# A two-layer decoder on one core: mask product issued once, silu as tanh, tables and gates earlier, a new order in the second attention

## The chip, the cores and the metric

The kernel runs on one core of a Trainium2 chip. Its time is the device time of one execution in microseconds (us). The core has five engines that each take their instructions strictly in order: PE (TensorE, matrix products and transposes; its weight loads are listed as PEld), DVE (VectorE), ACT (ScalarE), POOL (GpSimd) and SP (SyncE, which issues most DMAs). They wait for one another through semaphores. The kernel's work is described in the order of its Python code, and a scheduler fixes the order in which each engine gets its instructions when the program is built, so a change of the code can move instructions that it does not mention.

## The reference

Everything is float32. Four sequences of 256 tokens, 256 wide, go through two decoder layers; each layer adds three blocks to `x`, with a layer norm before each.

```python
x = x + L0_attn(ln(x))            # 8 heads, 2 key/value heads, 32 wide, window of 64, tanh soft cap
x = x + L0_xattn(ctx, ln(x))      # state-space scan over ctx (16 states), gated by silu(ln(x))
x = x + L0_ffn(ln(x))             # 704 wide, silu(g) * u
x = x + L1_attn(ln(x))            # 16 heads, 4 key/value heads, 128 wide, causal
x = x + L1_xattn(ctx, ln(x))      # a second scan, gated
x = x + L1_ffn(ln(x))             # 32 experts, 6 chosen for each token, and a shared one
```

The parts that the change touches, cut to the core:

```python
# L0_attn, after rotating q and k and normalising q, k and v
scores = jnp.where(allowed, q @ k.T / sqrt(D), -inf)
probs = softmax(tanh(scores / 30) * 30)
# scan: for each time step t, with 256 channels and 16 states
state = state * exp(d_t * A) + (d_t * u_t) * B_t
y_t = (state @ C_t) + D * u_t           # then y * silu(z), z = ln(x)
# L0_ffn
g = (xf @ gate_w.T) * gate_s
u = (xf @ up_w.T) * up_s
out = ((silu(g) * u) @ down_w.T) * down_s
# L1_attn
q = layernorm(q, qn_g, qn_b);  k = layernorm(k, kn_g, kn_b)
q = q * cos + rotate_half(q) * sin      # the same for k
weights = softmax(where(causal, -inf, q @ k.T / sqrt(D)))
x_add = concat_heads(weights @ v) @ w_o.T
```

## The kernel before

`x` lies in SBUF for the whole program, eight blocks of 128 tokens. The work runs through these stages, and the two scans are threaded through the others as generators that yield after each state.

**Layer 0's attention** (from L340, batches 0 to 3). `head0` normalises and projects a batch and rotates q and k: for each half `c` of the batch it writes the product with cos to SBUF, the product of the swapped halves with sin to SBUF, and after both halves one add over both joins them. `tail0` makes the scores. For each of two key/value heads and each pair of heads it takes two PSUM tiles, puts the window's mask into them as a product of an identity with the table `far` (bfloat16, L432), and then adds the score products (L436) on top. The mask product runs three times in a row into the same two tiles; each starts the tile afresh, so the last one alone decides what lies there. Then ACT takes tanh and exp, PE the weighted values, DVE divides.

**The scan** (`mamba_front` from L150, `mamba_scan` from L202). For each state and half of the channels: ACT takes an exponential into PSUM (`h`, L215), POOL forms `db` (L217), DVE runs the scan in place (L218) and multiplies by C (`hc`, L220). In layer 0 PE sums the even states in PSUM by a product with the identity (L235) and POOL adds the odd ones to `y` (L237); in layer 1 POOL adds all (L227). The front of a scan also uses silu (`u`), softplus (`dt`) and exp (`negA`) on ACT. Where ACT goes from a function of one table set to one of another, the program has a table load, which the profile lists as an ACT row without a tile.

**The gate** (`mamba_gate`, L246). For a batch: layer-norm statistics of `x` (DVE, then four small POOL steps), silu on ACT (`sz`, L252), a product with the scan's `y` on DVE (`yg`), four transposes (L258), an add to `x` (L264).

**Feed-forward** (L541 to L587). Two halves of two batches each. A half gates its batches, normalises and transposes them, and runs six chunks of the inner width (`ic`). Each chunk has two PSUM tiles, gate `pg` and up `pu`, from a pool of two (`pb`); L554 fills them with four matmuls of 512 columns each for gate and up (a float32 product is two passes); ACT takes silu of `pg` with the gate's scale (L562), and DVE multiplies it by `pu` and the up scale into `hT` (L565). Then the down matmuls (L578, 48 records) and the add to `x` (L586). The second half begins once the layer-0 scan `s01` has run to its end.

**Second attention** (L590 to L821, loop L1009 to L1029). At its start POOL builds the rotary tables with the norms' weights folded in (`cg`, `sg`, `bt`, L602 to L621), PE transposes one of them (L629), and the mean of the q and k weights over a head has been taken out (`wmean`, L520 to L524, one reduce over all 20 heads, and two subtractions on POOL). For each batch `keys_values` (L687) normalises the batch, projects and rotates its keys. For each of its four key/value heads, a step, `queries` (L680) projects, rotates and transposes both halves of four query heads: `rotate` (L652) takes squares on ACT (L658) and three passes on DVE (L663, L670, L671), `transposed` (L674) four transposes (L677) and a copy. `rsqrt` (L632) is one step on DVE (L635) and a power on POOL (L636). `scores` (L735) makes scores (L741, L750), adds offsets and mask on DVE (L759), takes the negative maximum (`nm`), the exponential with its sum on ACT (L769), the reciprocal of the sums on DVE (L772), and scales on POOL (L774). `weighted` (L777) transposes (L784 the first) and multiplies with the values; `project_out` (L807) runs after every second step and adds to `x` (L820). The loop keeps two steps in flight, in this order:

```python
xnT, kT = keys_values(b)
for g in range(NKV1):
    rq = queries(xnT, g, qT)
    queued.append((b, g, qT, rq, kT, xnT))
    if len(queued) > 1: score()
    if len(scored) > 1: finish()
    with tc.issue_after(pace[-3]) ...: run(states, ...)   # some states of layer 1's scan
```

`score` makes the scores of the step before, `finish` the weighting of the step before that. `pace` holds the reciprocals, and the scan's states of a step may not be issued before the third last of them.

**Mixture of experts** (`moe`, from L904): for each expert up (L944), gate and square (L949, L950) and down (L958). Its routing and first products begin before the second attention ends.

## Time and profile before

| | us |
|---|---|
| median of 3 runs | 913.7 (910.06 to 918.71) |
| the profiled execution | 913.37 |
| its span | 911.6 |
| mean granted clock of PE | 0.941 |

Busy time over the span: PE 805.6 us (88%), its weight loads 500.7, DVE 585.5 (64%), ACT 485.9 (53%), POOL 422.3 (46%). A busy time counts records from start to end, and those of PE overlap and are modelled, so PE at 88% is not PE at its peak. Averages over the whole span say little here, since each stage has another limit. The stages lie about so: layer 0's attention 0 to 200, feed-forward 212 to 314 (first half 212 to 257, second 279 to 314), second attention 321 to 665, experts 665 to the end.

The chain of waits, which follows the work that ended last back from the end, gives PE 52% of the span, DVE 15%, ACT 7%, POOL 5% and starts for which nothing was waited 4%. The page's groups of instructions have one row for a line, engine and shape: count, busy time, mean duration in ns, then the idle time of that engine just before, and who ended most of it. In a list of the chain, the columns are the start and the length in us, then engine, tile, line and count.

### The profile page before, as it was taken

What the parts mean: (1) busy time and instruction counts of PE and PEld (TensorE: products, weight loads), DVE (VectorE), ACT (ScalarE), POOL (GpSimd) and SP (SyncE); (2) the same over time, 40 slices, a digit from 0 to 9 for tenths busy, and PEclk for the clock granted to TensorE, in tenths of its full rate; (3) what the DMA queues carried; (4) which work ended last, traced back from release to release, by engine and by line L of the source; (5) the groups of instructions that cost most, each with busy time, mean ns of one, the idle gap of its engine ahead of it and who ended that gap; (6) DMA issues with size and microseconds to landing.
All of it is one profiled execution on the core that took longest, in us unless ns stands there. A gap on an engine that the chain in (4) does not pass through costs nothing.

```text
span 911.6 us, 10272 instructions
## 1 busy us (share of the span) xinstructions
PE 805.6 (88%) x3074; PEld 500.7 (55%) x3074; DVE 585.5 (64%) x1096; ACT 485.9 (53%) x1191; POOL 422.3 (46%) x421
## 2 busy tenths in 40 slices
PE   4888789978968789889898978997999999999997
PEld 1444456633434435646564755675666656666665
DVE  3799797677867268979669874777256776221221
ACT  2768453778869346757765664776523343211111
POOL 3366866467759334847656652332347661000000
PEclk9999787987988989999999989997999999999999
DMA  4357354464532200101111110000137653555442
GB/s 160 117 152 268 105 184 162 145 216 152 200 115 92 86 30 24 46 24 47 46 47 56 38 35 12 24 3 1 49 116 228 226 151 112 159 143 154 161 148 81
DMA packets 60999, 98.36 MB, mean 108 GB/s; under 512 B 6336, under 2 KB 26704, under 8 KB 60688
## 3 DMA queue, kind: packets, MB, share of 16 engines
q1 hardware_dynamic: 59232, 95.77, 33.0%
q10 hardware_dynamic: 1712, 1.94, 0.7%
q8 instruction: 24, 0.39, 0.2%
q14 instruction: 31, 0.25, 0.1%
HBM read 96.24 MB, written 1.44 MB: 107 GB/s over the span
## 4 chain that ended last, share of the span: by engine, by line
PE 52%; DVE 15%; ACT 7%; POOL 5%; issue 4%; DMA 1%; POOLq 0%; SPq 0%; DVEq 0%; ACTq 0%
PE ps L944 12%; PE ps L958 12%; PE ps L812 5%; PE ps L554 4%; PE ps L643 4%; PE ps L578 2%; PE ps L750 2%; DVE h L218 2%; PE ps L797 2%; DVE ps L670 1%; DVE qs L663 1%; ACT sc L769 1%; DVE hc L220 1%; DVE qr L671 1%; PE ps L677 1%
## 5 line engine op out<-in xcount | busy, mean ns | idle before, releaser
L217 POOL TENSOR_TENSOR db<-bt,du 128x512 f32<-128x512 f32 x128 | 163.5, 1290 | 86.6 <-DVE h L218 64.3
L218 DVE TENSOR_TENSOR_SCAN h<-h,db 128x512 f32<-128x512 f32 x128 | 152.5, 1216 | 17.6 <-ACT h L215 16.0
L958 PE MATMUL ps<-w,hT 128*128 128x256 f32 x544 | 128.8, 380 | 0.0
L944 PE MATMUL ps<-moe_xnT,w 128*128 128x512 f32 x272 | 128.8, 597 | 0.0
L949 DVE SCALAR_TENSOR_TENSOR hT<-ps,gr 128x512 f32<-128x512 f32 x64 | 44.1, 689 | 127.0 <-PE ps L944 127.0
L958 PEld LDWEIGHTS ps<-w,hT 128*128 128x128 f32 x544 | 103.3, 191 | 40.3 <-issue 29.4
L215 ACT ACTIVATE h<-dt,negA 128x512 f32<-128x512 f32 x128 | 86.5, 689 | 62.6 <-DVE hc L220 61.9
L950 ACT ACTIVATE hT<-hT 128x512 f32<-128x512 f32 x68 | 42.8, 629 | 134.1 <-DVE hT L949 133.9
L643 PE MATMUL ps<-wqkv,xnT 128*128 128x512 f32 x192 | 95.7, 611 | 7.6 <-DVE rq L635 4.1
L220 DVE TENSOR_TENSOR hc<-h,ct 128x512 f32<-128x512 f32 x128 | 84.9, 679 | 4.1 <-POOL y L237 2.1
L227 POOL TENSOR_TENSOR y<-y,hc 128x512 f32<-128x512 f32 x64 | 80.8, 1272 | 8.0 <-DVE hc L220 8.0
L636 POOL TENSOR_TENSOR rq<-rq,nhalf 128x8 f32<-128x8 f32 x20 | 33.0, 1648 | 90.6 <-DVE rq L635 90.4
L944 PEld LDWEIGHTS ps<-moe_xnT,w 128*128 128x128 f32 x272 | 51.7, 191 | 36.5 <-issue 33.2
L658 ACT ACTIVATE sq<-ps 128x128 f32<-128x128 f32 x160 | 42.4, 282 | 41.3 <-PE ps L643 37.9
L769 ACT ACTIVATE sc<-sc,nm 128x256 f32<-128x256 f32 (+1 forms) x128 | 56.7, 449 | 12.3 <-DVE nm L764 8.2
L774 POOL TENSOR_TENSOR sc<-sc,rsum 128x512 f32<-128x512 f32 (+1 forms) x32 | 46.3, 1468 | 35.3 <-DVE rsum L772 33.6
L812 PE MATMUL ps<-wo,oT 128*128 128x256 f32 x256 | 57.0, 381 | 0.4 <-ACT oT L805 0.4
L812 PEld LDWEIGHTS ps<-wo,oT 128*128 128x128 f32 x256 | 48.1, 190 | 9.2 <-ACT oT L805 2.6
L235 PE MATMUL ps<-hc,ident 128*128 128x512 f32 x64 | 39.9, 712 | 13.9 <-DVE hc L220 10.9
L643 PEld LDWEIGHTS ps<-wqkv,xnT 128*128 128x128 f32 x192 | 33.8, 195 | 30.3 <-issue 20.7
L677 PE MATMUL ps<-ident,qr 128*128 128x128 f32 x160 | 28.9, 299 | 18.4 <-DVE qr L671 16.2
L237 POOL TENSOR_TENSOR y<-y,hc 128x512 f32<-128x512 f32 x32 | 40.8, 1275 | 7.6 <-DVE hc L220 6.3
(200 smaller groups left out, 1449.2 us busy)
## 6 DMA issues: line engine op xcount, KB each, us to landing
bt<-bc SPq DMA_DIRECT2D x96, 256.0 KB, 3.5
ct<-bc SPq DMA_DIRECT2D x96, 256.0 KB, 3.6
w<-in_w_dram SPq DMA_DIRECT2D x64, 256.0 KB, 3.6
gr<-gt SPq DMA_DIRECT2D x64, 256.0 KB, 3.5
wqkv<-in_wqkv_dram SPq DMA_DIRECT2D x1, 3072.0 KB, 14.1
wo<-in_wo_dram SPq DMA_DIRECT2D x1, 2048.0 KB, 8.1
x<-in_x_dram SPq DMA_DIRECT2D x4, 256.0 KB, 5.3
w<-in_ws_dram SPq DMA_DIRECT2D x4, 256.0 KB, 3.2
```

Source lines behind the costliest of these rows:

```text
L215: nc.scalar.activation(h, dt[:, c, :], AF.Exp, scale=negA[:, a : a + 1])
L217: nc.gpsimd.tensor_mul(db, bt, du[:, c, :])
L218: nc.vector.tensor_tensor_scan(h, h, db, 0.0, ALU.mult, ALU.add)
L220: nc.vector.tensor_mul(hc, h, ct)
L227: nc.gpsimd.tensor_add(y[:, c, :], y[:, c, :], state(n, c, bt, ct))
L643: mm(pq, lhsT=xnT[:, f, c * P : (c + 1) * P], rhs=wqkv1[:, f, ch * 512 : (ch + 1) * 512], start=(f == 0), stop=(f == 1),)
L769: nc.scalar.activation(part, part, AF.Exp, bias=nm[:, qc, j : j + 1], accum_out=rsum[:, qc, j : j + 1])
L774: nc.gpsimd.tensor_mul(part, part, rsum[:, qc, :].unsqueeze(2).to_broadcast([P, 4, w]))
L812: mm(pout[:, c * 256 : (c + 1) * 256], lhsT=oTs[h // 4][:, h % 4, c * P : (c + 1) * P], rhs=wo1[:, 8 * gp + h, :], start=(h == 0), stop=(h ...
L944: mm(ph_, lhsT=w[:, f * P : (f + 1) * P], rhs=xnT[:, f, :], start=(f == 0), stop=(f == 1))
L949: gated.append(nc.vector.scalar_tensor_tensor(h, ph_, 0.0, g, ALU.max, ALU.mult).ins)
L958: mm(po[t // 2][:, (t % 2) * 256 : (t % 2 + 1) * 256], lhsT=h[:, t * P : (t + 1) * P], rhs=w[:, 256:512], start=start and t % 2 == 0, stop ...
```

## The change

The mask product in `tail0` is issued once instead of three times. The rotation of layer 0 multiplies by cos in place in PSUM and adds for each half. The rotary tables of the second attention are built before feed-forward's code, in a pool that lives for the whole program, and the weights' mean is taken in four pieces of five heads. `mamba_gate` is split: `gates_of` has the statistics and the silu, and in feed-forward both batches' `gates_of` stand ahead of the rest of `s01`. Feed-forward's silu becomes a tanh: silu(g) is g/2 times (1 + tanh(g/2)), so ACT takes a tanh with half the scale, a new DVE step forms (1 + tanh) times `pg`, and the multiplier of the last step is the product of half the gate's scale and the up scale (`both`). In the second attention `queries` rotates both halves before it transposes either; `keys_values` of the next batch is called after step 1 of a batch; the reciprocal of the sums is a power of −1 on POOL, and `pace` takes the second maximum instead; the add to `x` after `project_out` is put off to the start of the next `finish` (`settle`).

Left out of the diff below are a renamed constant (`R_KG` is `R_1`, the same column) and the list `owed` among the loop's lists.

```diff
@@ -95,2 +95,4 @@
     nc.gpsimd.memset(nhalf, -0.5)
+    minus = cpool.tile([P, 8], F32, name="minus")
+    nc.gpsimd.memset(minus, -1.0)
     dpool = ctx.enter_context(tc.tile_pool(name="dpool", bufs=1, space=bass.MemoryType.DRAM))
@@ -245,13 +247,20 @@
-    def mamba_gate(l, b, pool):
+    def gates_of(b, pool, bufs):
         nb, rs = ln_stats([x[:, 2 * b + c, :] for c in range(2)])
-        pt = ps(pool)
+        szs = []
         for c in range(2):
-            sz = work.tile([P, S], F32, tag="sz", name="sz")
+            szs.append(pool.tile([P, S], F32, tag="sz", name="sz", bufs=bufs))
             nc.scalar.activation(
-                sz, x[:, 2 * b + c, :], AF.Silu, bias=nb[:, c : c + 1], scale=rs[:, c : c + 1]
+                szs[c], x[:, 2 * b + c, :], AF.Silu, bias=nb[:, c : c + 1], scale=rs[:, c : c + 1]
             )
+        return szs
+    def mamba_gate(l, b, pool, szs=None):
+        szs = szs or gates_of(b, work, 2)
+        pt = ps(pool)
+        for c in range(2):
             yg = work.tile([P, S], F32, tag="yg", name="yg")
-            nc.vector.tensor_mul(yg, y_of[l, b // 2][:, c, (b % 2) * S : (b % 2 + 1) * S], sz)
+            nc.vector.tensor_mul(yg, y_of[l, b // 2][:, c, (b % 2) * S : (b % 2 + 1) * S], szs[c])
             for lh in range(2):
@@ -358,3 +367,2 @@
                 q3 = pq[:, 0:320].rearrange("p (h d) -> p h d", d=32)
-                nc.vector.tensor_mul(r[:, c, 0:10, :], q3, cos.unsqueeze(1).to_broadcast([P, 10, 32]))
                 nc.vector.tensor_mul(
@@ -364,2 +372,5 @@
                 )
+                nc.vector.tensor_mul(q3, q3, cos.unsqueeze(1).to_broadcast([P, 10, 32]))
+                nc.vector.tensor_add(r[:, c, 0:10, :], q3, rr[:, c])
                 nc.scalar.copy(
@@ -367,3 +378,2 @@
                 )
-            nc.vector.tensor_add(r[:, :, 0:10, :], r[:, :, 0:10, :], rr)
@@ -427,7 +437,4 @@
                     psc = [ps(pb) for _ in range(2)]
-                    for last in range(3):
-                        for p_ in psc:
-                            mm(p_[:, 0:320], lhsT=identb, rhs=far, start=True, stop=(last < 2))
+                    for p_ in psc:
+                        mm(p_[:, 0:320], lhsT=identb, rhs=far, start=True, stop=False)
                     for klo, qlo, lo, hi in ((0, 0, 0, NEAR), (P, P, NEAR, 320)):
@@ -518,8 +525,34 @@
+    tabs = []
+    for gcol, bcol in ((R_QG, R_QB), (R_1, R_KB)):
+        g_ = row[:, gcol - R_BR : gcol - R_BR + D1]
+        b_ = row[:, bcol - R_BR : bcol - R_BR + D1]
+        cg = cpool.tile([P, 2, D1], F32, name=f"cg{gcol}")
+        sg = cpool.tile([P, 2, D1], F32, name=f"sg{gcol}")
+        bt = cpool.tile([P, 2, D1], F32, name=f"bt{gcol}")
+        bs = cpool.tile([P, 2, D1], F32, tag="bs", name="bs")
+        cos = cst1[:, 0:256].rearrange("p (c d) -> p c d", c=2)
+        sin = cst1[:, C_SIN1 - C_COS1 : C_SIN1 - C_COS1 + 256].rearrange("p (c d) -> p c d", c=2)
+        nc.gpsimd.tensor_mul(cg, cos, g_.unsqueeze(1).to_broadcast([P, 2, D1]))
+        nc.gpsimd.tensor_mul(bt, cos, b_.unsqueeze(1).to_broadcast([P, 2, D1]))
+        for lo, hi in ((0, 64), (64, 0)):
+            for dst, v in ((sg, g_), (bs, b_)):
+                nc.gpsimd.tensor_mul(
+                    dst[:, :, lo : lo + 64],
+                    sin[:, :, lo : lo + 64],
+                    v[:, hi : hi + 64].unsqueeze(1).to_broadcast([P, 2, 64]),
+                )
+        nc.gpsimd.tensor_add(bt, bt, bs)
+        tabs.append((cg, sg, bt))
     wh = wqkv1[:, :, 0 : 20 * D1].rearrange("p f (h d) -> p f h d", d=D1)
     wmean = cpool.tile([P, 2, 20], F32, name="wmean")
-    nc.vector.tensor_reduce(wmean, wh, AX.X, ALU.add)
-    nc.vector.tensor_scalar(wmean, wmean, 1.0 / D1, None, ALU.mult)
-    for f in range(2):
-        nc.gpsimd.tensor_sub(wh[:, f], wh[:, f], wmean[:, f, :].unsqueeze(2).to_broadcast([P, 20, D1]))
+    for h in range(0, 20, 5):
+        hs = slice(h, h + 5)
+        nc.vector.tensor_reduce(wmean[:, :, hs], wh[:, :, hs], AX.X, ALU.add)
+        nc.vector.tensor_scalar(wmean[:, :, hs], wmean[:, :, hs], 1.0 / D1, None, ALU.mult)
+        for f in range(2):
+            nc.gpsimd.tensor_sub(
+                wh[:, f, hs], wh[:, f, hs], wmean[:, f, hs].unsqueeze(2).to_broadcast([P, 5, D1])
+            )
@@ -538,2 +571,8 @@
+        halfg = wp.tile([P, NIC], F32, name="halfg")
+        both = wp.tile([P, NIC], F32, name="both")
+        nc.gpsimd.tensor_scalar(halfg, par[:, P_GATES : P_GATES + NIC], 0.5, None, ALU.mult)
+        nc.gpsimd.tensor_mul(both, halfg, par[:, P_UPS : P_UPS + NIC])
         conv_taps(1)
@@ -541,2 +580,3 @@
         for hf in range(2):
+            szs = [gates_of(2 * hf + bb, fp, 4) for bb in range(2)]
             if hf == 1:
@@ -545,3 +585,3 @@
             for bb in range(2):
-                mamba_gate(0, 2 * hf + bb, pc)
+                mamba_gate(0, 2 * hf + bb, pc, szs[bb])
                 ln_transposed(2 * hf + bb, xnT[:, :, bb * S : (bb + 1) * S], pc)
@@ -560,13 +600,11 @@
                         )
                 sg = fp.tile([P, 512], F32, tag="sg", name="sg")
-                nc.scalar.activation(
-                    sg[0:m, :], pg[0:m, :], AF.Silu, scale=par[0:m, P_GATES + ic : P_GATES + ic + 1]
+                nc.scalar.activation(sg[0:m, :], pg[0:m, :], AF.Tanh, scale=halfg[0:m, ic : ic + 1])
+                nc.vector.scalar_tensor_tensor(
+                    sg[0:m, :], sg[0:m, :], 1.0, pg[0:m, :], ALU.add, ALU.mult
                 )
                 nc.vector.scalar_tensor_tensor(
-                    hT[0:m, ic, :],
-                    pu[0:m, :],
-                    par[0:m, P_UPS + ic : P_UPS + ic + 1],
-                    sg[0:m, :],
-                    ALU.mult,
-                    ALU.mult,
+                    hT[0:m, ic, :], pu[0:m, :], both[0:m, ic : ic + 1], sg[0:m, :], ALU.mult, ALU.mult
                 )
@@ -599,24 +637,2 @@
-        tabs = []
-        for gcol, bcol in ((R_QG, R_QB), (R_KG, R_KB)):
-            g_ = row[:, gcol - R_BR : gcol - R_BR + D1]
...
-            tabs.append((cg, sg, bt))
         mask1 = cst1[:, C_MASK1 - C_COS1 : C_MASK1 - C_COS1 + 384]
@@ -679,8 +695,7 @@
-        def queries(xnT, g, qT):
+        def queries(xnT, g):
             ss = small.tile([P, 2, 4], F32, tag="qss", name="qss")
-            for c in range(2):
-                transposed(rotate(xnT, c, g, ss[:, c, :]), c, qT)
-            return rsqrt(ss, qks)
+            qrs = [rotate(xnT, c, g, ss[:, c, :]) for c in range(2)]
+            return qrs, rsqrt(ss, qks)
@@ -764,3 +779,3 @@
             nc.vector.tensor_reduce(nm[:, 0, :], sc[:, :, 0:P], AX.X, ALU.max, negate=True)
-            nc.vector.tensor_reduce(nm[:, 1, :], sc[:, :, P:384], AX.X, ALU.max, negate=True)
+            pace.append(nc.vector.tensor_reduce(nm[:, 1, :], sc[:, :, P:384], AX.X, ALU.max, negate=True).ins)
             rsum = small.tile([P, 2, 4], F32, tag="rsum", name="rsum")
@@ -771,3 +786,3 @@
                     )
-            pace.append(nc.vector.reciprocal(rsum, rsum).ins)
+            nc.gpsimd.tensor_tensor(rsum, rsum, minus[:, 0:8].rearrange("p (c h) -> p c h", c=2), ALU.pow)
             for qc, part, w in ((0, sc[:, :, 0:P], P), (1, sc[:, :, P:384], 256)):
@@ -818,4 +833,8 @@
                     )
-            xb = x[:, 2 * b : 2 * b + 2, :]
-            nc.vector.tensor_add(xb, xb, pout.rearrange("p (t d) -> p t d", t=2))
+            owed.append((x[:, 2 * b : 2 * b + 2, :], pout))
+        def settle():
+            for xb, pout in owed:
+                nc.vector.tensor_add(xb, xb, pout.rearrange("p (t d) -> p t d", t=2))
+            owed.clear()
@@ -1008,12 +1028,17 @@
         ready = None
+        keyed = [keys_values(0)]
         for b in range(B):
-            xnT, kT = keys_values(b)
+            xnT, kT = keyed.pop(0)
             for g in range(NKV1):
+                qrs, rq = queries(xnT, g)
                 qT = ap.tile([P, 4, S], F32, tag="qT", name="qT", bufs=2)
-                rq = queries(xnT, g, qT)
-                queued.append((b, g, qT, rq, kT, xnT))
-                if len(queued) > 1:
+                for c in range(2):
+                    transposed(qrs[c], c, qT)
+                if queued:
                     score()
+                queued.append((b, g, qT, rq, kT, xnT))
                 if len(scored) > 1:
                     finish()
+                if g == 1 and b + 1 < B:
+                    keyed.append(keys_values(b + 1))
                 step = 4 * b + g
@@ -1024,2 +1049,3 @@
                 if step == 12:
+                    settle()
                     for bb in range(2):
@@ -1034,2 +1060,3 @@
             finish()
+        settle()
```

By count the built program goes from 1834 to 1770 matmul instructions, from 71 to 40 table loads on ACT, from 26 to 10 reciprocals on DVE and from 349 to 372 two-operand steps on POOL; DVE gets twelve more of the product that the tanh needs. The DMAs are the same in number. In the built order of POOL the tables' 14 steps stand between the first layer norms and the first `krep` of layer 0's attention.

## The prediction

> **What bounds the kernel now.** I read the page's slices first, then windows cut at the stage borders, then the chain of waits inside the stages that the change touches. The slices (each 22.8 us) say which engine fills which stage:
> ```profile
> PE   4888789978968789889898978997999999999997
> ...
> DVE  3799797677867268979669874777256776221221
> ...
> PEclk9999787987988989999999989997999999999999
> ```
> PE carries most of the span, but only the last third (mixture of experts, which the change leaves alone) is solid. Windows by stage; columns are length, then busy time (x instructions) of PE, its weight loads, DVE, ACT and POOL, then granted clock:
> ```profile
> 40.00:100.00 60.00, 49.22 (x210) 26.75 (x211) 58.91 (x94) 43.61 (x79) 37.20 (x36) 0.95 0.59 195
> 100.00:140.00 40.00, 32.86 (x159) 21.76 (x157) 32.35 (x51) 16.26 (x36) 31.93 (x24) 0.80 0.47 155
> 140.00:182.00 42.00, 40.40 (x222) 27.46 (x222) 27.94 (x39) 25.34 (x53) 23.35 (x19) 0.90 0.48 156
> 212.00:257.00 45.00, 44.12 (x118) 21.70 (x118) 37.39 (x45) 38.29 (x45) 33.58 (x29) 0.95 0.62 203
> 257.00:279.00 22.00, 11.44 (x28) 3.91 (x28) 14.35 (x38) 15.14 (x22) 10.43 (x26) 0.67 0.22 67
> 279.00:314.00 35.00, 33.95 (x96) 17.12 (x94) 17.70 (x24) 24.68 (x26) 20.86 (x20) 0.96 0.18 60
> 321.00:595.00 274.00, 242.96 (x987) 155.57 (x988) 210.81 (x401) 174.85 (x654) 147.86 (x126) 0.96 0.11 33
> ```
> So DVE bounds 40-100 (58.9 of 60), PE bounds 140-182 and both feed-forward halves (212-257, 279-314), the gap between the halves (257-279) is latency, with PE busy for half of it at clock 0.67, and in attention 1 PE idles 274 − 243 = 31 us with no other engine full. Times below are against the profiled execution: span 911.6, 913.4 with what lies around it, 0.3 under the median 913.7.
>
> **Mask product.** 64 of 96 products go. The chain shows six of them pipelined, 0.135 each:
> ```profile
> 171.98 0.81 PE ps L432 x6
> ```
> That is 64 × 0.135 = 8.6 us of PE work. Only in 140-182 is PE the bound; about half of the products lie there: 32 × 0.135 = 4.3, of which some is returned as waits on ACT's tanh. I take −3; bounds −8.6 (all on the path) and, leaving the clock to a rival below, 0.
> In-place rotation: one add per batch (1.19 us) becomes two of about 0.48 (the row of the multiplies beside it): −0.24 × 4 = −1 us of DVE, inside the uncertainty of the −3. The mean of the second attention's weights (a 5.46 us reduce, two 4.46 us subtractions) is cut in four with the same elements: no sum changes; the pieces sit among scan states, and were that cover gone, the most is eight more instruction starts, under 1 us.
>
> **Feed-forward, silu as tanh.** ACT now swaps function tables for every inner chunk, because scan's exponentials lie between silus:
> ```profile
> 227.48 1.28 ACT L562
> ...
> 229.49 1.28 ACT L215
> 230.78 0.70 ACT h L215
> ```
> In the whole program 71 loads become 40 by the built code's count, 31 × 1.283 = 39.8 us of ACT, nowhere the fullest engine. On the path stands one stretch in the first half: PE ends at 227.42 and starts again at 234.56 (two loads, sg, h, then DVE's scan), 7.1 us; the half's opening L554 x8 takes 5.79 where later ones take 3.43, 2.4 more for the clock. Against it: each chunk gains one DVE product in two steps, 12 × 0.75 (L565's row) = 9.0 us, and the gate's PSUM buffer, one of two, is held for tanh 0.69 + 0.75 = 1.44, against the 1.72 that PE needs for the other half of the chunk: it fits by 0.28, if DVE comes at once. Queued on DVE ahead of it may be a scan step (h 1.22, hc 0.68); behind it scan steps wait 0.75 each time, and for those PE's state sums (L235) and POOL's. In the built order of after, the states sit behind the first half's L554, and more run in the gap.
> The gap: early gates take two sz, three table loads (1.28 each) and a second statistics chain out of the 17.9 us from 260.40 to 278.29; about 5 us, less what DVE puts between (three h and two hc by the order, 5.0). DVE's floor for 212-279 is 51.7 + 6 × 0.75 = 56.2 of 67, so −11 is the most this stretch could give while DVE is full. I take −6; and for the second half (PE's matmuls fill all but 1.9 of 35; its last chunk trades a 1.28 load for a 0.75 product) −1.5. Bounds for both: −15, and +10 (9.0 of products wholly on the path, plus 1).
>
> [...]
>
> **Tables of the second attention.** At the border PE waits for 14 POOL steps, two transposes, and only then projects:
> ```profile
> 314.25 0.73 POOL cg L611
> ...
> 317.98 0.69 POOL bt L620
> ...
> 318.72 0.69 PE ps L629 x2
> ...
> 321.06 1.22 PE ps L643
> ```
> After's order has the 14 steps at POOL's start, ahead of the first krep, where POOL waits 18.7 us for DVE; they are about 7.5 us and are covered; without the cover they'd delay the scan's first db by as much. Their two DMAs keep their place on ACT's queue. L629 and the layer norm of batch 0 move into the second half's PE stream; what is next is L643 straight after the last L578. Of 314.14 to 321.06 = 6.9 I take −6.5; bounds −7 and −4.5 (layer norm 318.72 to 321.06 stays).
>
> **Second attention's order.** A batch starts with keys, all in one chain:
> ```profile
> 388.49 1.73 PE ps L643 x4
> ...
> 390.30 1.15 ACT sq L658 x8
> ...
> 394.06 1.66 POOL rq L636
> ...
> 397.70 1.10 PE ps L643 x2
> ```
> PE's chain is broken from 390.22 to 397.70, 7.5 us; three times (batches 1 to 3) 22.5. With keys projected a step and a half earlier other PE work covers them. The keys' own instructions (DVE about 10 us a batch: four passes of 0.70 and 0.60 each, eight L696 of 0.3) stay, and stand on DVE and ACT ahead of that step's scan. I take two thirds, −15. The reciprocal leaves DVE, where it waited 17.6 us in all for ACT's exponentials with rotations queued behind it; some reach PE (L677 waits 16.2 on qr): −5. Both rotations ahead of both transposes keep PE's second projection off the first's wait; small, inside this. The add to x, issued a step later, stands in the order right ahead of L759s that need PE's next work anyway: 0; were that cover gone, 8 adds of 0.70 either way, 5.6, inside the bounds. Sum −20. Bounds: all idle PE time of 321-665, 31 + 7.6 = −38.6, and +8 (L677 waiting half as long again, since it now needs both rotations).
> The reciprocal on POOL has this row as nearest (same size, power):
> ```profile
> L636 POOL TENSOR_TENSOR rq<-rq,nhalf 128x8 f32<-128x8 f32 x20 | 33.0, 1648 | 90.6 <-DVE rq L635 90.4
> ```
> 16 × 1.65 = 26.4 us; POOL is at 148 of 274, and the scaled scores usually lie ready 8 us before PE takes them (end 431.6, L784 at 440.07). Behind it on POOL wait the scaling and scan's db. At the last step nothing covers it (L784 waits 1.54 for POOL at 648.37): +1.6; bounds 0 and +3.3 (two steps).
>
> **Sum**: −3 − 6 − 1.5 − 6.5 − 20 + 1.6 = −35.4; 913.4 − 35.4 = 878.
>
> **Rivals.**
> Stalls go wholly: attention at −38.6 instead of −20, and −3 more in feed-forward: 913.4 − 57 = 856. For it: no engine there is full. Against: DVE, in one order, meets PE four times a step.
> Order brings nothing in the second attention: the next wait (qs on sq, scores on DVE) takes the place of the keys' chain. Left are −6.5, −3 in feed-forward and −3, +1.6: 902.5. For it: L820, L677, L735 all end on DVE, which keeps its 211 us.
> No change: attention turns +8, tables and gates pay for it: about 912.
> Slower, the clock: the two extra rounds of mask products also keep PE busy while ACT works. In 40-182 PE is busy 122.5 us at a mean 0.89. At 0.55 the same work takes 122.5 × 0.89 / 0.55 = 198, 56 over the 142 there is; less the other 32 gained, 913.4 + 24 = 937. It decides from the point where the loss is 32: 122.5 × 0.89 / 174 = a granted clock of 0.63. For it: 100-140 is already at 0.80, 257-279 at 0.67. Against: only 8.6 us of work goes, and half the stage waits for DVE, not PE.
> [...]
>
> **How the numbers follow.** Chances: forecast (865 to 893) 0.48, stalls go wholly 0.14, nothing from the order (894 to 909) 0.20, no change 0.06, clock 0.12. A measurement of this kernel tells about 1% from no change, 904.3 and 922.5. Faster: 0.48 + 0.14 + 0.15 = 0.77; within: 0.05 + 0.06 + 0.01 = 0.12; slower 0.11. The range takes in all but the deepest cases below (0.04) and the clock and part of no change above (0.16): 850 to 912.
>
> **What would show it.** Right: PE's first L643 of the second attention follows the last down product within 2 us; periods from one batch's first project_out to the next (428.69, 512.88, 595.14: 84.2 and 82.3) fall to about 77; the gap between the halves is under 15 us; no L562 loads in ACT's row. Wrong: PE waits on DVE's new product in L554, by more than 0.3 a chunk; granted clock under 0.7 in 100-182; key projections stuck behind DVE, so that PE idles mid-batch for as long as it did at the border; PE L784 waiting for POOL in more than two steps.

## The result, and the profile after

| | before | changed |
|---|---|---|
| median of the runs | 915.8 us (4 runs) | 926.0 us (4 runs) |
| ratio to before | 1 | 1.013, 95% interval 1.008 to 1.018 |
| span of the profiled execution | 911.6 us | 926.3 us |
| its mean granted clock of PE | 0.941 | 0.922 |

The changed kernel is 1.3% slower; the forecast was 3.9% faster, and the time lies above the range. The page's slices (each 23.2 us) and the shares of its chain:

```profile
PE   4898999978974987898798889997899999999997
...
DVE  4699785757768458988797587767237676312211
...
PEclk9988766969975999999999999997999999999999
...
PE 50%; DVE 14%; POOL 13%; issue 7%; ACT 3%; DMA 2%; SPq 0%; POOLq 0%; DVEq 0%; ACTq 0%
```

Two things stand out beside the page of before: the 7, 6, 6 in the clock's row between 93 and 162 us, where before has 7, 8, 7; and POOL at 13% of the chain, before 5%. To place the difference I laid the starts and ends of the same instructions of both traces side by side (us from the start of the span):

| | before | changed | moved by |
|---|---|---|---|
| last add of layer 0's attention | 186.5 | 182.0 | −4.5 |
| first half's first up product | 212.6 | 204.5 | −8.1 |
| first half's last down product ends | 257.1 | 246.2 | −10.9 |
| the layer-0 scan's four sums into `y`: second | 158.3 | 162.5 | +4.2 |
| third | 220.4 | 240.6 | +20.2 |
| fourth | 260.4 | 275.8 | +15.4 |
| second half's first up product | 278.3 | 295.5 | +17.2 |
| second half's last down product ends | 314.1 | 332.1 | +18.0 |
| second attention's first projection | 321.1 | 332.9 | +11.9 |
| its last output product ends | 664.9 | 679.8 | +14.9 |
| end of the span | 911.6 | 926.3 | +14.7 |

So attention and the first half did get earlier, by as much as 11 us. It is given back with interest in the gap between the halves, which grew from 21.2 to 49.3 us, because the second half waits for the scan to be finished, and the scan was late. The border to the second attention gave what was forecast, 7.0 to 0.8 us, and the second attention lost 3. In all +18.0 − 6.1 + 3.0, and −0.2 in the experts, make the 14.7 us of the span. In windows (length, then busy time (x instructions) of PE, weight loads, DVE, ACT and POOL, then granted clock, DMA share, GB/s):

```profile
100.00:160.00 60.00, 56.53 (x230) 39.39 (x230) 44.97 (x73) 25.91 (x66) 38.33 (x33) 0.63 0.45 139
204.00:249.00 45.00, 41.89 (x111) 19.56 (x109) 30.91 (x39) 16.50 (x25) 22.44 (x20) 0.95 0.43 133
249.00:276.00 27.00, 18.61 (x33) 6.59 (x32) 18.53 (x24) 15.09 (x19) 20.19 (x17) 0.82 0.56 198
276.00:295.50 19.50, 5.76 (x16) 2.25 (x15) 16.13 (x35) 10.26 (x17) 12.77 (x21) 0.50 0.51 182
333.00:605.00 272.00, 236.63 (x978) 149.12 (x978) 214.23 (x391) 170.96 (x650) 165.06 (x135) 0.99 0.11 34
```

In the first half (204 to 249) DVE is busy for 31 of 45 us, where before it was busy for 37: there was room for scan steps (the in-place scan on DVE, L220), but only 7 stand among the half's products, 10 before. The others stand in 249 to 276. Then 276 to 295.5 is nearly empty of PE work at clock 0.50. The chain there (start, length, what):

```profile
278.32 0.69 DVE x L273
...
282.50 1.09 ACT xn L138 x2
...
284.81 1.24 DVE h L220
...
286.13 1.26 POOL db L219
287.39 1.23 POOL y L229
288.62 1.24 POOL db L219
...
290.24 3.94 DMA w<-in_ws_dram
...
294.40 0.60 ACT xn L138
...
295.52 2.08 PE ps L594 x2
```

L229 is the scan of layer 1. Its first states already stand on POOL's and DVE's queues ahead of the layer norm of the last batch, which the second half needs. The chain's longest piece, a DMA, was inferred; the rows of the engines in order of time show what this norm waits for:

```profile
286.69 1.22 DVE L220 TENSOR_TENSOR_SCAN h<-h,db 128x512 f32<-128x512 f32 x1
...
287.82 0.67 DVE L273 TENSOR_TENSOR x<-x,ps 128x512 f32<-128x512 f32 x1
...
289.80 1.26 POOL L229 TENSOR_TENSOR y<-y,hc 128x512 f32<-128x512 f32 x1
...
291.13 0.22 POOL L126 TENSOR_SCALAR ln_nb<-ln_mv 128x2 f32<-128x2 f32 x1
...
292.74 1.09 ACT L138 ACTIVATE xn<-x,ln_nb,ln_rs 128x256 f32<-128x256 f32 x2 [2.92 <-POOL ln_nb L129]
```

The gate's add to `x` (L273) comes behind a scan step, and the norm's steps on POOL behind an add of the scan, about 1 us each time; `xn` at 292.74 is the last batch's, the one at 294.40 belongs to a later norm. Taking sz and three table loads out of this gap, as forecast, was real (no silu stands in this chain), but from the fourth sum to the first up product it is still 19.8 us, where before had 17.9. So 15.4 of the second half's 17.2 us are the scan's lateness and 1.9 this path.

At the border:

```profile
326.08 6.04 PE ps L616 x24
332.12 0.82 issue
332.94 1.97 PE ps L659 x4
```

The projection follows the last down product after 0.82 us: this step of the forecast is right.

### The profile page after: what moved, and what is told of

Read it like the earlier page. It is cut to its first block, busy times and chain, and to the rows that moved or that the text cites. A ratio compares the mean times of both kernels' runs of the same rounds, so it can differ in the third digit from the quotient of the medians.

```text
span 926.3 us, 10124 instructions
## 1 busy us (share of the span) xinstructions
PE 817.0 (88%) x3010; PEld 502.8 (54%) x3010; DVE 591.8 (64%) x1102; ACT 445.0 (48%) x1160; POOL 448.4 (48%) x446
## 4 chain that ended last, share of the span: by engine, by line
PE 50%; DVE 14%; POOL 13%; issue 7%; ACT 3%; DMA 2%; SPq 0%; POOLq 0%; DVEq 0%; ACTq 0%
PE ps L963 12%; PE ps L977 12%; DVE h L220 3%; PE ps L827 3%; PE ps L594 3%; POOL db L219 3%; POOL y L229 3%; PE ps L659 2%; PE ps L237 2%; POOL sc L789 2%; POOL rq L652 2%; DMA ct<-bc 1%; PE ps L616 1%; PE ps L812 1%; PE ps L443 1%
## 5 line engine op out<-in xcount | busy, mean ns | idle before, releaser
L219 POOL TENSOR_TENSOR db<-bt,du 128x512 f32<-128x512 f32 x128 | 161.6, 1274 | 115.1 <-DVE h L220 94.8
L220 DVE TENSOR_TENSOR_SCAN h<-h,db 128x512 f32<-128x512 f32 x128 | 152.6, 1216 | 17.8 <-ACT h L217 17.7
L977 PEld LDWEIGHTS ps<-w,hT 128*128 128x128 f32 x544 | 103.4, 191 | 40.4 <-issue 29.4
L229 POOL TENSOR_TENSOR y<-y,hc 128x512 f32<-128x512 f32 x64 | 80.7, 1271 | 4.7 <-DVE hc L222 4.6
L237 PE MATMUL ps<-hc,ident 128*128 128x512 f32 x64 | 44.0, 785 | 11.1 <-DVE hc L222 11.0
L693 PE MATMUL ps<-ident,qr 128*128 128x128 f32 x160 | 28.2, 292 | 17.2 <-DVE qr L687 13.4
```

Of the source, the lines that this page charges most:

```text
L219: nc.gpsimd.tensor_mul(db, bt, du[:, c, :])
L220: nc.vector.tensor_tensor_scan(h, h, db, 0.0, ALU.mult, ALU.add)
L229: nc.gpsimd.tensor_add(y[:, c, :], y[:, c, :], state(n, c, bt, ct))
L237: mm(yp, lhsT=ident, rhs=hc, start=(n == 0), stop=(n == 14))
L977: mm(po[t // 2][:, (t % 2) * 256 : (t % 2 + 1) * 256], lhsT=h[:, t * P : (t + 1) * P], rhs=w[:, 256:512], start=start and t % 2 == 0, stop ...
```

## The experiments

Each was timed beside runs of the kernel before on the same chip, with ten runs, e2, e4, e7 and e12 with four. Ratios are to that kernel, so the changed kernel stands at 1.013 (1.008 to 1.018). e1 to e4 are each the changed kernel with one part as it was. Times of single instructions are from one profile of each kernel.

**e1: late gates.** In feed-forward's loop:

```diff
-            szs = [gates_of(2 * hf + bb, fp, 4) for bb in range(2)]
             if hf == 1:
                 run(s01)
...
-                mamba_gate(0, 2 * hf + bb, pc, szs[bb])
+                mamba_gate(0, 2 * hf + bb, pc)
```

> The changed kernel with feed-forward's gates back where they were (statistics and silu inside the gate, behind the rest of the layer-0 scan). Theory order: calling the gates early lets the scheduler put scan states behind the first half of feed-forward; DVE's built order has 23 scan steps between the last product of the first half and the first of the second, against 10 before the change and 12 in this kernel. Then the last layer-0 state sum (275.8 us in the changed kernel, 260.4 before) comes back to about 263, and the total to about 913. Theory clock: the scan is late because PE's clock fell in layer 0's attention; then the sum stays at 275 and the total at 925.

Measured: 1.006 (1.003 to 1.010), 923.1 us. The fourth sum comes at 268.7, the down products end at 322.9, 9 us earlier than in the changed kernel, 9 later than before. The sum came back by 7 of the 13 us that theory order said; the second sum (167.2) is late as in the theory of the clock. Neither alone, and by the medians the interval overlaps the changed kernel's.

**e2: three masks.** The loop over three rounds again in L432's place.

> The changed kernel with the mask product issued three times again. Theory clock: the granted clock in 100 to 160 us, 0.63 in the changed kernel and 0.79 before, goes back above 0.75, the last layer-0 state sum falls by 10 us or more, total 915 or less. Theory order: the clock may rise, but the sum falls by 4 us at most, total 921 to 926.

Measured: 1.020 (1.012 to 1.028), 933.7 us, slower than the changed kernel. The granted clock in 100 to 160 went up to 0.80 and the second sum to 155.6, earlier than before, and still the fourth came at 276.6. A higher clock does not help here: with 21 scan steps between the halves by the built order, the scan's end is late all the same.

**e3: the reciprocal on DVE**, and the scan's states paced by it again instead of by the second maximum (that line is left out here):

```diff
-            nc.gpsimd.tensor_tensor(rsum, rsum, minus[:, 0:8]..., ALU.pow)
+            pace.append(nc.vector.reciprocal(rsum, rsum).ins)
```

> The changed kernel with the reciprocal of the sums on DVE again, and the scan's states paced by it. Theory POOL: in the second attention POOL's steps are 24% of the chain (before, the scaling alone at 2.5%), since the power and its wait for ACT stand ahead of the scan on POOL and take back what the earlier keys gave; then the stage from the first L659 to the last L827 falls from 346 to about 335 us and the total to about 915. Theory DVE: the stage is bound by DVE's work and the order gains nothing; then it stays within 3 us and the total at 925.

Measured: 1.006 (1.001 to 1.010), 922.2 us; the stage takes 340.7 us instead of 346.8. What POOL waits for in the second attention (total us, times, longest), in the changed kernel:

```profile
POOL rq L652 <- DVE rq L651: 53.0, 10, 8.2
POOL db L219 <- DVE h L220: 37.9, 11, 6.4
POOL rsum L787 <- ACT sc L784: 22.7, 4, 10.0
```

and in e3:

```profile
POOL sc L789 <- DVE rsum L787: 60.5, 11, 12.0
POOL rq L652 <- DVE rq L651: 51.4, 10, 8.2
POOL db L219 <- DVE h L220: 15.2, 8, 4.4
```

In the changed kernel the power waits 22.7 us for the exponentials at the head of POOL's queue, with the scan's db behind it. But in e3 the scaling in its place waits even longer for the reciprocals, 60.5 us; what gets shorter is db's wait for DVE's scan steps. So power and pacing together cost about 6 us here, where +1.6 was forecast for the power: theory POOL in the outcome, though the stage came to 341 and not to 335. Which of the two costs it is not shown.

**e4: keys late.** `xnT, kT = keys_values(b)` at the start of each batch again.

> The changed kernel with each batch's keys projected at the start of the batch again. Theory POOL: the earlier keys do give time, which something else takes back; then this costs about 10 us, total about 935. Theory DVE: the earlier keys give nothing, total 925 within 3.

Measured: 1.021 (1.014 to 1.029), 934.2 us; the stage takes 350.3 instead of 346.8. The earlier keys come out as 3.5 us by the profile and some 7 by the medians. The sign is that of theory POOL, with a gain well below the 15 of the forecast. It is not clear of the noise: the intervals overlap, and the four kernels with power and early keys (the changed one, e1, e2, e12) take 344.2 to 351.4 for the stage.

**e5: masks, gates and reciprocal undone** (the diffs of e1 to e3 together).

> The changed kernel with three parts undone: mask product three times, gates late, reciprocal on DVE. Left of the change: tanh, tables, rotation, mean in four pieces, keys and queries in the new order. Built order: 9 scan steps between the halves on DVE. Theory order and clock together: with late gates alone the state sums still lag by 9 us at 167 us, which the three masks took away where they were tried (155.6); so the last state sum comes back to 260, the down products end at 312 to 314, the second attention takes 340, and the total is about 905. Theory tanh: the lag that late gates leave comes from the product that tanh adds on DVE; then the last sum stays at 266 or later and the total at 913 or more.

Measured: 1.002 (0.997 to 1.007), 917.8 us. Missed: expected was about 905. The fourth sum comes at 275.1, as late as in the changed kernel, though only 9 scan steps stand between the halves; the granted clock in 100 to 160 is 0.61 with three mask rounds. So neither the count of steps nor the rounds alone tell where the scan ends. In time this is what theory tanh said, but tanh alone (e8, e15 below) costs less.

**e6: layer 0 and feed-forward as before**, reciprocal on DVE; left of the change are the tables, the keys, the order of queries and the late add.

> The changed kernel with layer 0 and feed-forward as before (three masks, old rotation, mean in one piece, silu, late gates) and the reciprocal on DVE; left are the early tables, early keys, the order of queries and the late add. Built order of the scan on DVE is that of before. Theory order: everything up to the end of feed-forward is as before (down products end at 314, within 2), K starts within 1 us of it, the second attention takes 341; total 913.4 - 6 - 3 = 904 to 906, faster than both. Theory POOL: tables at the start of POOL's queue delay the scan; then the down products end 5 us or more later and the total is 911 or more.

Measured: 0.992 (0.988 to 0.995), 908.2 us, span 901.2: faster than both kernels, and the best found. The down products end at 314.3 as before, the projections start 0.8 later, the stage takes 339.0.

**e7: the kernel before with one mask round.**

> The kernel before with the mask product issued once, nothing else. Theory clock: granted clock in 100 to 160 falls from 0.79 to about 0.63 and the scan's second state sum moves from 158 to about 167; the total rises by 5 to 9, to about 920 on the scale where the kernel before has 914. Theory PE work: 8.6 us of PE work less, the total falls by 2 to 4.

Measured: 1.014 (1.006 to 1.021), 928.3 us. Clock 0.62, second sum 167.5, fourth 275.6: theory clock, with a larger loss than it said. One line, which removes work, makes the kernel before as slow as the whole change. But two things differ: the clock, and the built order, which has 14 scan steps between the halves instead of 10. The next four hold one of them.

**e9 and e10: clock or order.** At the end of the program, every engine's instructions are chained in the order in which another kernel was built, so that the scheduler has no choice:

```diff
+    for e, order in held.items():
+        for a, b in zip(order, order[1:]):
+            tc.add_manual_dep(per[e][b], per[e][a].name, no_sync, reason="hold")
```

e9 is the kernel before with one mask round in its own order; e10 has its three rounds in the order of e7.

> The kernel before with the mask product once, and every engine's instructions chained in the order in which the kernel before was built (64 products fewer on PE, nothing else moved). e7, where the scheduler was free, lost 1.4%. Theory clock: the removal itself is what costs, by the clock: granted clock in 100 to 160 near 0.62, scan's second state sum at 165 or later, ratio 1.008 or more. Theory order: the scheduler's other order is what cost in e7; here the ratio is 0.995 to 1.003.

> The reverse: the kernel before with its three mask rounds, in the order in which e7 was built (14 scan steps between the halves). Theory clock: granted clock about 0.8, ratio within 0.004 of 1. Theory order: the down products end at 325 or later, ratio 1.01 to 1.02.

Measured: e9 1.007 (1.004 to 1.010), e10 1.002 (0.999 to 1.006). So the removal costs 0.7% in the old order, clear of the noise, and 1.2% in the new one (e10 to e7, where the intervals touch). The new order costs 0.2% with three rounds and 0.7% with one, neither clear of the noise. e9 has theory clock's sign but not its figures: 0.76 and not 0.62 in 100 to 160, and the second sum at 158.8; the sum that comes late is the fourth, 266.6 where before has 260.4. Windows of before:

```profile
40.00:100.00 60.00, 49.22 (x210) 26.75 (x211) 58.91 (x94) 43.61 (x79) 37.20 (x36) 0.95 0.59 195
100.00:160.00 60.00, 52.35 (x255) 35.19 (x254) 47.10 (x73) 24.93 (x58) 44.06 (x33) 0.79 0.47 158
```

and of e9, whose engines have the same instructions in the same order but for the 64 products:

```profile
40.00:100.00 60.00, 51.72 (x183) 28.52 (x184) 54.93 (x90) 40.11 (x71) 33.42 (x35) 0.80 0.62 188
100.00:160.00 60.00, 51.36 (x228) 33.63 (x226) 49.27 (x75) 27.59 (x64) 47.08 (x34) 0.76 0.54 164
```

PE is busy for as long in e9 (103.1 of 120 us, before 101.6), though it has fewer products: each takes longer, at 0.80 and 0.76 instead of 0.95 and 0.79. Two rows of the same products between 40 and 182 us, before and in e9, show it (count, then busy time and mean ns):

```profile
L166 PE MATMUL ps<-ctxT,taps 128*128 128x512 f32 x32 | 17.2, 646 | 0.7 <-ACT dt L190 0.7
L490 PE MATMUL ps<-wo,attnT 128*128 128x256 f32 x24 | 5.9, 388 | 0.0
...
L166 PE MATMUL ps<-ctxT,taps 128*128 128x512 f32 x32 | 23.3, 850 | 1.2 <-ACT dt L190 1.2
L489 PE MATMUL ps<-wo,attnT 128*128 128x256 f32 x24 | 9.0, 543 | 0.0
```

The other pair agrees: 0.93 and 0.89 in e10, 0.86 and 0.62 in e7.

**e11 and e12: the same pair elsewhere.** e11 is e6 with one round, e12 the changed kernel with three, each in the order of its partner.

> The kernel of e6 with the mask product once, in the order in which e6 was built. Theory order: 8.6 us of PE work less, of it 0 to 4 on the path: ratio to the kernel before 0.988 to 0.992. Theory clock: ratio 1.000 or more.

> The changed kernel with three mask rounds, in the order in which the changed kernel was built (23 scan steps between the halves). Theory clock: granted clock in 100 to 160 back near 0.8, last state sum earlier by 5 us or more, ratio 1.007 or less. Theory order: ratio as the changed kernel's 1.013 or up to 0.006 more.

Measured: e11 0.999 (0.997 to 1.002), against e6's 0.992: the removal costs 0.8% there too, and the fourth sum moves from 256.9 to 265.3. e12 1.020 (1.011 to 1.028), against 1.013: in the changed kernel's own order three rounds are no better. There the fourth sum comes at 273.1, so 12.7 of the 15.4 us by which it is late stay with three rounds. The price of the removal is shown in two orders; in the changed kernel's own, where something else already makes the scan late, it does not show.

**e8, e13 to e17: the other parts, one at a time.** e8 puts the tanh into the kernel before; e13 to e17 put one part each into e6 (0.992): early gates, rotation and mean, tanh, mean alone, rotation alone.

> The kernel before with feed-forward's silu as a tanh, nothing else. As forecast: first half loses ACT's table swaps, gains DVE's product; up to the end of the down products 3 to 8 us less, total about 909. Theory tanh: DVE's added product delays scan and next chunk; the down products end 3 us or more later than 314, total 917 or more.

> e6 with the early gates alone. Built order: 14 scan steps between the halves instead of 10. Theory order: the state sums lag at the end and layer 1's states stand ahead of the second half's layer norm; the down products end at 320 or later (e6: 314.3), ratio to the kernel before 1.000 or more against e6's 0.992. As forecast (two silus and three table loads out of the gap): 2 to 5 us faster than e6, ratio 0.987 to 0.990.

> e6 with the new rotation and the mean in four pieces. Theory order: these move the scheduler's order in layer 0's attention, PE's granted clock in 100 to 160 falls below 0.7 as in e5 (0.61; e6 0.86), and the ratio is 0.998 or more. Otherwise (as forecast, nothing): 0.990 to 0.994.

> e6 with the tanh. Theory tanh: as in e8 the last state sum comes 6 us later, ratio 0.995 to 0.999. As forecast: 3 to 8 us faster than e6, ratio 0.983 to 0.988.

> e6 with the mean in four pieces alone. Built order: 48 scan steps ahead of the first feed-forward product and 8 between the halves (e6: 48 and 10). Theory order, by the rotation: nothing changes, ratio 0.989 to 0.994. Theory pieces: the small reductions among scan states cost; ratio 0.998 or more.

> e6 with the new rotation alone. Built order: 44 scan steps ahead of the first feed-forward product and 17 between the halves. Theory order, by the rotation: the scan lags, down products end at 319 or later, ratio 0.998 or more. Theory pieces: ratio 0.989 to 0.994.

| | ratio | interval | against its base | scan steps between the halves, built order |
|---|---|---|---|---|
| e8 before + tanh | 1.003 | 0.999 to 1.007 | +0.3% | 8 (before: 10) |
| e15 e6 + tanh | 0.996 | 0.992 to 1.000 | +0.4% | 8 (e6: 10) |
| e13 e6 + early gates | 0.993 | 0.990 to 0.997 | +0.2% | 14 |
| e16 e6 + mean in four | 0.996 | 0.991 to 1.000 | +0.4% | 8 |
| e17 e6 + rotation | 1.002 | 0.998 to 1.006 | +1.0% | 17 |
| e14 e6 + both | 1.003 | 0.998 to 1.008 | +1.2% | 13 |

None of these parts is a gain. The differences under 0.5% are within the intervals of e6 and of the kernel itself and say no more than that no gain of the forecast's size is there. The rotation's is clear of them: it turns one add of 1.23 us per batch into two of 0.48, 0.27 us less, and costs 1%. With it come another built order (44 scan steps ahead of the first feed-forward product instead of 48) and a granted clock of 0.72 instead of 0.86 in 100 to 160; which of these costs it is not shown. Of the expectations, e8, e15 and e17 came out in time as tanh and order had it; e14 did too, but without its sign (clock 0.80, not below 0.7), and e16 fell between its two. e13 missed both ways: the gates neither gain nor, alone, lose the 8 us that its one profile shows (fourth sum at 265.1, e6's at 256.9).

## Why the prediction was wrong

**The step that failed** is first the sum for layer 0 and feed-forward, −3 − 6 − 1.5 = −10.5, measured +18.0, and next the second attention's, below. I costed each edit on the old order and took the scan for cover. The scan is the work that ends last before the second half, and its moving stood in the sum at nothing. I had read in the built order that more states run in the gap and used it only as a deduction from the gates' gain. What the runs showed in its place: the scan's fourth sum comes 15.4 us later, the second half waits for it, and the gap between the halves, which was to lose about 5 us, grew by 28. The built order of DVE has 23 scan steps between the halves in the changed kernel and 10 before; that count was there to be taken without a chip. With the changed order held and the mask rounds restored (e12), 12.7 of the 15.4 us stay. The gates bring the count from 12 (e1) to 23, and without them the fourth sum is 7 us earlier; the rotation alone brings it to 17 (e17) and costs 1%.

But the count does not forecast the end of the scan by itself: e5 and e15, with 9 and 8 steps, have the fourth sum at 275.1 and 272.8, e10 with 14 at 262.9. Over the 19 profiles the fourth sum goes with the count at a correlation of 0.60 and with the granted clock in 40 to 160 at −0.70. So that the scan is late is shown, and that the edits of layer 0 and feed-forward make it late (e6); the shares of order and clock are shown for the mask product alone.

**The clock** was a rival at 0.12, with 24 us slower. That the removal costs time is shown with the order held: two rounds of products whose result is thrown away are worth 0.7% (before and e9) and 0.8% (e6 and e11), 6 to 7 us, and perhaps 1.2% (e10 and e7). That it goes by the clock is read from the rows: the same products take longer (in e9 850 ns for 646, and 543 for 388). The rival's price was too high, and it falls elsewhere. Its 0.55 for 40 to 182 was an assumption that no run shows: the lowest mean over 40 to 160 is 0.71 (e1 and e3). Its deciding point, 0.63 over 40 to 182, was not reached either; the granted clock there was 0.77, by the rival's own formula 122.5 × 0.89 / 0.77 = 142 us, just what there is. Attention's last two batches took 53.2 us in the changed kernel (128.8 to 182.0) and 54.6 before; it is the scan beside them that lags. My reason against the rival, that half the stage waits for DVE, holds for attention alone. In 140 to 182, where PE was busy for 40.4 of 42 us before, the granted clock fell too: from 0.90 to 0.76 with the order held (e9), though PE never waited longer than 1.0 us in it, and to 0.76 in the changed kernel, where its longest wait there is 0.18. And 64 × 0.135 = 8.6 us of PE work saved gave no gain clear of the noise in any order.

**Tanh**: the mechanism was named, the gain did not come. The loads went as counted: ACT's busy time fell from 485.9 to 445.0 us, 40.9, by the count 31 loads of 1.283 us each, 39.8. PE did not wait for the new product to speak of: in the changed kernel's row (idle before, and who ended it)

```profile
L594 PE MATMUL ps<-f_xnT,gw 128*128 128x512 f32 (+1 forms) x48 | 26.8, 686 | 2.9 <-DVE sg L605 1.9 <-ACT f_xnT L145 0.9
```

it is 1.9 us over twelve chunks, 0.16 each, under the 0.3 that I set as the sign of failure. But e8 and e15 show no gain (0.3% and 0.4% slower, within the noise): what ACT is freed of was worth nothing on the path, or DVE's new product (12 × 0.68 = 8.2 us in the changed kernel) took it back, since DVE also carries the scan. The later fourth sum (266.9 in e8, 260.4 before) speaks for the second; it is argued, not shown.

**Tables**: right, −6.1 for −6.5.

**Second attention**: −20 + 1.6 forecast, +3.0 measured; the periods between batches, which were to fall to about 77 us, are 86.1 and 83.8 (first output products at 435.3, 521.4 and 605.2). The keys' term was mis-sized: I counted the length of the chain between two key projections, 7.5 us, as idle PE, three times. The windows of before over the three starts of a batch say otherwise:

```profile
390.20:397.70 7.50, 5.84 (x19) 2.76 (x18) 5.41 (x12) 3.43 (x24) 1.65 (x1) 1.00 0.00 0
473.00:481.00 8.00, 6.73 (x21) 3.53 (x20) 4.26 (x9) 2.29 (x16) 1.65 (x1) 1.00 0.00 0
556.00:564.00 8.00, 6.48 (x20) 3.53 (x19) 4.12 (x8) 2.29 (x16) 0.91 (x1) 1.00 0.00 1
```

PE was busy for 19.05 of 23.5 us, with work that the chain does not list. There were 4.45 us to be had, and e4 shows 3.5, within the noise. The reciprocal's two terms were forecast at −5 for DVE and +1.6 for POOL, and together, with the pacing, they are +6.1 (346.8 against e3's 340.7). Without them the stage is some 2 us shorter than before: 339.0 to 345.5 in the nine profiles with early keys and the reciprocal on DVE, 342.0 to 343.8 in the five with the stage as before (medians 340.7 and 342.8). In e6 the longest waits of PE are DVE's:

```profile
PE ps L690 <- DVE qr L684: 14.3, 10, 5.4
PE ps L727 <- DVE e L728: 4.3, 2, 2.2
```

which was 16.2 for the rotation (qr) before; rotations on DVE still stand in front of PE, as the rival "order brings nothing" had it.

**Still open**: whether three rounds cost the changed kernel time in its own order (e12's four runs do not tell); how much of a part's effect is order and how much clock where the order was not held (e1, e5, e8, e13 to e17); and whether the power or the pacing costs the second attention its 6 us. The parts do not add up: from e6, one mask (+0.8%), gates (+0.2%), rotation (+1.0%), mean (+0.4%), tanh (+0.4%) and the power (+0.7%) would make 1.027, and the changed kernel has 1.013; several of the terms are within the noise. Early gates in an otherwise unchanged order were not tried.

## What to carry to other kernels

Where a scheduler makes the order, cost the new order, not the edit: count on each engine what stands ahead of the step that ends last (here scan steps between the halves) in both built programs before pricing any instruction, and take a large change there as a risk with a price, not as a forecast of the time. To learn what an edit itself is worth, hold the order and change only it. A chain's length is not an engine's idle time (here three stretches of 7.5 to 8 us held 4.45 us of idle PE in all): take the engine's busy time in the same window first. Moving a step to an idler engine moves its wait too (here the power waited 22.7 us in all at the head of POOL's queue), so price the wait with the step.

## What the runs showed of the hardware

The granted clock of one program differs from run to run, and the time goes with it. The ten runs of e14, time and mean clock of the whole span:

```
909.21 0.940   909.25 0.939   909.85 0.942   917.36 0.932   918.16 0.933
918.40 0.932   918.88 0.930   920.66 0.930   921.92 0.928   922.33 0.928
```

The correlation is −0.98 there, and between −0.74 and −0.99 in 15 of the 16 other timed experiments (e11: −0.43), some of them of four runs. By a straight line through the runs of each of these 16 kernels, 0.01 of mean clock goes with 3 to 10 us (e16: 902.2 at 0.955, 914 at 0.935; here 909.5 at 0.940, 919.5 at 0.930). Which of the two drives the other the correlation does not say. So one profile of a kernel is one draw: its time can be 9 us off the median (e14: 909.2, median 918.3), which is why the small parts above are judged by ratios over ten runs. The granted clock over 40 to 160 us was 0.71 to 0.78 in all seven profiles with one mask round, and 0.73 to 0.91 in the twelve with three. In the changed kernel PE never waited longer than 1.9 us between 100 and 182 us, and the granted clock there was 0.71, before 0.85 with waits of 2.9 and 2.2 us.
